# Ten state rows turned by ScalarE and TensorE, three C products on VectorE, and one state copy per pair of scans

## The chip, the cores and the metric

The kernel runs on one core of a Trainium2 chip. A core has five engines with a queue of their own each, worked off strictly in order: TensorE (PE: matrix products and transposes, results in PSUM), VectorE (DVE), ScalarE (ACT), GpSimd (POOL, which works on SBUF only in this kernel) and SyncE (SP, which issues nearly all DMAs). The metric is the device time of one launch in microseconds. Before the change it is 3146.35 us, the median of three runs from 3142.82 to 3151.95.

## The reference

The input `x` is (4, 512, 32, 32) in float32. Layer 0 normalises it by groups of channels and runs a selective state-space block over the 1024 pixels of each image; layer 1 is a block with two 3x3 convolutions and an attention over pixels. Only the recurrence of layer 0 matters to the change:

```python
xm, z = split(layernorm(tokens) @ W_in)               # 1024 channels each
xs = silu(causal_conv4(xm) + conv_b)
proj = xs @ W_x                                       # dt (32), B (16), C (16) per token
dt = softplus(proj[..., :32] @ W_dt + b_dt)
A = -exp(A_log)                                       # 1024 channels x 16 states
def step(h, inp):                                     # over the 1024 tokens
    dt_t, B_t, C_t, x_t = inp
    h = exp(dt_t * A) * h + (dt_t * x_t) * B_t        # h: channels x 16 states
    y = einsum('bds,bs->bd', h, C_t)
    return h, y
out = ((ys + xs * D_param) * silu(z)) @ W_out
```

## The kernel before, in words

**Tiling.** Channels lie on the 128 partitions, tokens along the free axis. A batch image has 8 chunks of 128 channels (`NDC`), taken two at a time (`e` = 0 to 3, `j` = 0, 1), and 1024 tokens, taken in two halves of 512 (`h` = 0, 1). So there are 4 x 4 x 2 = 32 groups `(b, e, h)`, and each holds 16 units, one for each state `s`. That makes 512 units and, with the two chunks, 1024 scans.

**One unit** (`unit`, L729 on). Each unit multiplies dt times x (`dtx`) by B, scans, multiplies by C and adds to y. B and C vary along the tokens and are the same on all partitions. The B product has two ways:

- *B on ScalarE* (`s in B_ON_ACT`): `dtx` has been transposed once per group (`dtxt`, tokens on partitions). ScalarE scales four pairs of rows by B (`sc`, L758, four instructions of 128x256), and TensorE turns them back into PSUM (`u`, L784, eight transposes). The decay exp(dt A) goes into an SBUF tile `da` of the ring `h` (L746).
- *B on GpSimd* (the other states): SP loads B spread over all partitions (`bbc`, 256 KB, L767), GpSimd multiplies (`dbx`, L773, 128x1024), and the decay goes into PSUM (`u`).

The scan over 512 tokens is one VectorE instruction per chunk (L798). In the half `h` = 0 a copy of the last element follows each scan (L803), into `carry_sb`, from which the scan of `h` = 1 starts. The C product again has two ways. For most states GpSimd multiplies both chunks at once by the loaded C (`cbc`, L820). For `s in C_ON_DVE` the scan writes to PSUM instead, and VectorE multiplies each chunk (L814, 128x512). Last, TensorE adds the result to `y` by transposing matmuls (L827, eight of 128x128).

**Rings.** `h` has 4 buffers for the states with B on ScalarE, `dbx` 4 for the others, `u` 4 PSUM banks, `sc` 2, `cbc` 6, `bb` 3. A buffer of `h` or `dbx` is free when TensorE has added it to `y`.

**The order of work.** `Plan` (L47 on) holds every piece of layer 0 as a step with an engine, an assumed duration in us, a priority, and the buffers it reads and writes. `issue` replays these durations and each time issues, among the steps that could start within `SLACK` of the soonest, the one of lowest priority number. So the order in every queue follows the assumed durations (`SCAN`, `EXP`, `ROWS`) and the priorities, which `PRM` spreads for the work beside the units: the next batch's normalisation (`m0`, `nl`), its projections and convolution taps (`q0`, `qg` for batch 1; `c0`, `cg` later), its parameters (`p0`), gates (`gates`), the previous batch's output projection (`o0`, `og`), the first image of layer 1 (`fi`), and, as filler, 32 weight transforms for layer 1 (`transform`, L1092 to L1106 on GpSimd). A step is only ordered here; at run time its engine waits on semaphores for whatever is not yet done, and everything behind it waits too.

Of the kernel before, what the change touches and what calls it, by code (L numbers as in the profile page):

```python
# [21 lines left out]
NS = 16  # L22
RK = 32
T = 512
# [3 lines left out]
GS = 16  # L28


PRM = dict(fi=0.66, m0=45.27, n0=50.77, nl=2.07, q0=63.18, qg=6.23, c0=53.17, cg=7.07, p0=122.02, e0=6.38, eg=3.72, g0=78.98, gg=9.04, o0=14.48, og=5.23, dl=9.01, t0=10, tg=21.42)


class Buf:
# [21 lines left out]
class Plan:  # L56
# [2 lines left out]

    ENGINES = ("PE", "DVE", "ACT", "POOL", "SP")  # L60
    LAG = {"PE": 0.2, "DVE": 0.08, "ACT": 0.1, "POOL": 0.06, "SP": 0.0}
    HOP, LOAD, SLACK, AHEAD = 0.05, 1.3, 0.07, 17.64

    def __init__(self, slots, in_order):
        self.slots, self.steps = dict(slots), []
# [104 lines left out]
def mamba_then_pab_kernel(  # L170
# [25 lines left out]
    nc = tc.nc  # L196
# [67 lines left out]
    with ExitStack() as l0:  # L264
# [10 lines left out]
        NPC = NCC * C // QC  # L275
        halves = [slice(h * T, (h + 1) * T) for h in range(NH)]

        B_ON_ACT = (0, 2, 4, 6, 8, 10, 12, 14, 15)

        C_ON_DVE = (1, 5, 9, 13)  # L280

        mean_w = wp.tile([P, P], F32, tag="mean_w", name="mean_w")
        nc.vector.memset(mean_w, 1.0 / C)
# [53 lines left out]
        )  # L337
        step = plan.step
        MM, TR = 0.88, 0.114
        ROWS, EXP, SCAN = 0.8, 0.62, 1.13  # L340

        def buf(ring, shape, name, free=False):
            if ring is None:
# [14 lines left out]

        proj = [buf(None, proj_sb[k * NP : (k + 1) * NP], "") for k in range(2)]
        bts = [buf(None, bt_sb[k], "") for k in range(2)]  # L360
        carry = [[buf(None, None, "") for j in range(2)] for s in range(NS)]
        bcds = [buf(None, t, "") for t in bcd]
        szds = [[buf(None, None, "") for d in range(NDC)] for b in range(B)]
        gds = [[[buf(None, None, "") for h in range(NH)] for k in range(2)] for b in range(B)]
# [319 lines left out]
        def delta(b, e, h, prio):  # L684

            pr = proj[b % 2]
            hs = halves[h]
            name = f"{b}_{e}_{h}"
            dt = buf("dt", [P, 2, T], f"dt_{name}")
            for j in range(2):  # L690
                d = 2 * e + j
                wd = wdt_sb[b % 2][:, d * P : (d + 1) * P]
                pd = group(f"pd_{name}_{j}", [(lambda wd=wd: wd, lambda: proj_sb[:, hs], [pr])], prio)
                step(
                    "ACT", 0.58,
                    lambda d=d, j=j, pd=pd: nc.scalar.activation(
                        dt()[:, j], pd(), AF.Identity, bias=bdt_sb[:, d : d + 1]
                    ),
                    [pd], [dt], prio,
                )  # L700
            step(
                "ACT", 0.97, lambda: nc.scalar.activation(dt(), dt(), AF.Softplus),
                [], [dt], prio, "softplus",
            )
            dtx = buf("dtx", [P, 2, T], f"dtx_{name}")
            us = [xs[b, 2 * e + j] for j in range(2)]

            def times():
                for j in range(2):
                    nc.gpsimd.tensor_mul(dtx()[:, j], dt()[:, j], us[j]()[:, hs])  # L710

            step("POOL", 2.37, times, [dt, *us], [dtx], prio)
            dtxt = buf("dtxt", [P, NK, 2, P], f"dtxt_{name}")
            for j in range(2):
                pt = buf("mm", [P, NK, P], f"pdt_{name}_{j}")

                def turn(j=j, pt=pt):
                    for k in range(NK):
                        nc.tensor.transpose(pt()[:, k, :], dtx()[:, j, k * P : (k + 1) * P], ident)

                step("PE", 4 * TR, turn, [dtx], [pt], prio)
                step(
                    "ACT", 0.48, lambda j=j, pt=pt: nc.scalar.copy(dtxt()[:, :, j, :], pt()),
                    [pt], [dtxt], prio,
                )
            dts[b, e, h] = dt, dtx, dtxt

        def unit(b, e, h, s, y):


            dt, dtx, dtxt = dts[b, e, h]
            hs = halves[h]
            name = f"{b}_{e}_{h}_{s}"
            prio = (b * NDC + 2 * e + h) * NS + s
            bc = bcds[b]
            c_bc = buf("cbc", [P, 1, T], f"cbc_{name}")
            step(
                "SP", 0.32,
                lambda: nc.sync.dma_start(c_bc()[:, 0], bcd[b][NS + s][hs].partition_broadcast(P)),
                [bc], [c_bc], prio, kb=256,  # L740
            )
            us = [buf("u", [P, T], f"u_{name}_{j}") for j in range(2)]

            def decay(j, t):
                at = (2 * e + j) * NS + s
                nc.scalar.activation(t, dt()[:, j], AF.Exp, scale=a_sb[:, at : at + 1])  # L746

            on_act, on_dve = s in B_ON_ACT, s in C_ON_DVE
            if on_act:
                bt = bts[b % 2]  # L750
                sc = buf("sc", [P, NK, 2, P], f"sc_{name}")
                hc = buf("h", [P, 2, T], f"da_{name}")
                for r in range(2):

                    def rows(r=r):
                        for k in range(2 * r, 2 * r + 2):
                            at = h * NK + k
                            nc.scalar.activation(  # L758
                                sc()[:, k], dtxt()[:, k], AF.Copy, scale=bt()[:, at, s : s + 1]
                            )  # L760

                    step("ACT", ROWS, rows, [dtxt, bt], [sc], prio)
            else:
                b_bc = buf("bb", [P, 1, T], f"bbc_{name}")
                step(
                    "SP", 0.32,
                    lambda: nc.sync.dma_start(b_bc()[:, 0], bcd[b][s][hs].partition_broadcast(P)),  # L767
                    [bc], [b_bc], prio, kb=256,
                )
                hc = buf("dbx", [P, 2, T], f"dbx_{name}")  # L770
                step(
                    "POOL", 2.31,
                    lambda: nc.gpsimd.tensor_mul(hc(), dtx(), b_bc().to_broadcast([P, 2, T])),  # L773
                    [dtx, b_bc], [hc], prio,
                )

            parts = [buf(None, None, "") for j in range(2)]
            for j, u in enumerate(us):
                part = parts[j]
                if on_act:  # L780

                    def turn(j=j, u=u):
                        for k in range(NK):
                            nc.tensor.transpose(  # L784
                                u()[:, k * P : (k + 1) * P], sc()[:, k, j, :], ident
                            )

                    step(
                        "ACT", EXP, lambda j=j: decay(j, hc()[:, j]), [dt], [part], prio, "exp",
                        holds=[hc],  # L790
                    )
                    step("PE", 4 * TR, turn, [sc], [u], prio - 1)
                else:
                    step("ACT", EXP, lambda j=j, u=u: decay(j, u()), [dt], [u], prio - 1, "exp")

                def scan(j=j, u=u):
                    ht = u() if on_dve else hc()[:, j]
                    nc.vector.tensor_tensor_scan(  # L798
                        ht, *((hc()[:, j], u()) if on_act else (u(), hc()[:, j])),
                        carry_sb[:, j, s : s + 1] if h else 0.0, ALU.mult, ALU.add,  # L800
                    )
                    if h == 0:
                        nc.vector.tensor_copy(carry_sb[:, j, s : s + 1], ht[:, T - 1 : T])  # L803

                step(
                    "DVE", SCAN if h else SCAN + 0.07, scan,
                    [part, u, *([carry[s][j]] if h else [])] if on_act
                    else [hc, u, *([carry[s][j]] if h else [])],
                    [u if on_dve else part, *([] if h else [carry[s][j]])], prio - 1, holds=[hc],
                )  # L810
                if on_dve:
                    step(
                        "DVE", 0.6,
                        lambda j=j, u=u: nc.vector.tensor_mul(hc()[:, j], u(), c_bc()[:, 0]),  # L814
                        [u, c_bc], [part], prio, holds=[hc],
                    )
            if not on_dve:
                step(
                    "POOL", 2.31,
                    lambda: nc.gpsimd.tensor_mul(hc(), hc(), c_bc().to_broadcast([P, 2, T])),  # L820
                    [c_bc], parts, prio, holds=[hc],
                )
            for j in range(2):

                def add(j=j):
                    for k in range(NK):
                        nc.tensor.matmul(  # L827
                            y[j]()[:, k, :], hc()[:, j, k * P : (k + 1) * P], ident,
                            start=(s == 0 and k == 0), stop=(s == NS - 1 and k == NK - 1),
                            is_transpose=True, skip_group_check=True,  # L830
                        )

                step("PE", 4 * TR, add, [parts[j]], [y[j]], prio, holds=[hc])
# [712 lines left out]
```

## Time and profile before

| | |
|---|---|
| median of three runs | 3146.35 us |
| profiled execution, its own time | 3149.88 us |
| its span | 3148.1 us (1.8 us of launch around it) |
| granted TensorE clock | 0.965 |
| start, before the first units | 0 to about 140 us |
| layer 0, units | about 140 to 2094 us |
| layer 1 | about 2094 to 3148 us |

The units end with the copy of the last `y` at 2093.68 to 2095.1 us. To read such a profile, look at each stage by itself: the shares of busy time over the whole span mix a stage in which four engines share the work with one in which TensorE does nearly all. An instruction's duration here includes a latency that the next one on the same engine can overlap. Where the cost of one more is wanted, the busy time of a group divided by its count, or the distance between starts in the timeline, is the better number. The "idle before" of a group and the list of waits name what ended an idle stretch.

### The profile page before, as it was taken

How to read it: one execution, taken by the hardware profiler on the slowest of the kernel's cores; microseconds unless marked ns; L12 is line 12 of the kernel's file. 1: busy time of each engine (PE TensorE's matmuls, PEld its weight loads, DVE VectorE, ACT ScalarE, POOL GpSimd, SP SyncE). 2: the span in 40 equal slices, each digit the busy share in tenths (PEclk: the TensorE clock that was granted, in tenths of full speed). 3: DMA queues.
4: the chain of work that ended last, by engine and by line, in shares of the span. 5: the costliest groups of instructions: out<-in, count | busy, mean ns of one | idle time of the engine just before them, and what ended most of it. 6: DMA issues, size and time to landing. Idle time of an engine off the chain costs nothing. (4 is left out here: it accounts for less than half of the span.)

```text
span 3148.1 us, 36186 instructions
## 1 busy us (share of the span) xinstructions
PE 2791.6 (89%) x11576; PEld 1642.3 (52%) x11576; DVE 2314.3 (74%) x3018; ACT 1859.4 (59%) x3198; POOL 2181.9 (69%) x1207
## 2 busy tenths in 40 slices
PE   4988789989889999888899877779999999999998
PEld 2455556656556656566656555444444444444443
DVE  3488999979998988898987888877285365447344
ACT  3499889997789998789998776652030030030000
POOL 8899997899978899978899998763152142224222
PEclk9999999999899999999999989989999999999999
DMA  6667555488645578745567654357268448628816
GB/s 195 194 188 216 152 159 166 142 249 242 208 122 168 173 214 248 227 127 163 162 193 222 212 179 127 118 146 262 92 233 313 175 158 309 254 82 308 318 68 245
DMA packets 406021, 608.41 MB, mean 193 GB/s; under 512 B 47688, under 2 KB 242504, under 8 KB 381256
## 3 DMA queue, kind: packets, MB, share of 16 engines
q1 hardware_dynamic: 396736, 590.52, 59.0%
q10 hardware_dynamic: 8936, 15.31, 1.3%
q8 instruction: 93, 1.52, 0.2%
q14 instruction: 96, 0.79, 0.1%
q0 software_dynamic: 160, 0.26, 0.0%
HBM read 508.99 MB, written 96.99 MB: 192 GB/s over the span
## 5 line engine op out<-in xcount | busy, mean ns | idle before, releaser
L820 POOL TENSOR_TENSOR da<-da,cbc 128x1024 f32<-128x1024 f32 x288 | 680.6, 2367 | 106.2 <-DVE carry_sb L803 54.3
L773 POOL TENSOR_TENSOR dbx<-dtx,bbc 128x1024 f32<-128x1024 f32 x224 | 528.6, 2371 | 24.8 <-DMA bbc<-bcd 10.8
L758 ACT ACTIVATE sc<-dtxt,bt_sb 128x256 f32<-128x256 f32 x1152 | 504.5, 497 | 48.0 <-PE u L784 46.8
L746 ACT ACTIVATE da<-dt,a_sb 128x512 f32<-128x512 f32 x576 | 394.3, 713 | 60.8 <-PE y L827 60.3
L784 PE MATMUL u<-ident,sc 128*128 128x128 f32 x2304 | 353.8, 286 | 72.5 <-DVE da L798 46.5
L798 DVE TENSOR_TENSOR_SCAN da<-da,carry_sb,u 128x512 f32<-128x512 f32 x288 | 356.2, 1263 | 73.6 <-PE u L784 71.1
L798 DVE TENSOR_TENSOR_SCAN da<-da,u 128x512 f32<-128x512 f32 x288 | 349.1, 1212 | 43.6 <-PE u L784 41.0
L827 PE MATMUL y<-ident,da 128*128 128x128 f32 x2304 | 326.4, 287 | 59.8 <-POOL da L820 56.5
L784 PEld LDWEIGHTS u<-ident,sc 128*128 128x128 f32 x2304 | 277.1, 146 | 181.2 <-DVE da L798 50.7
L827 PEld LDWEIGHTS y<-ident,da 128*128 128x128 f32 x2304 | 276.4, 147 | 163.1 <-POOL da L820 122.0
L1383 PE MATMUL m_b<-uw_b,v_b 128*128 128x512 f32 x768 | 336.0, 594 | 10.3 <-DMA uw_b<-u_b 8.6
L746 ACT ACTIVATE u<-dt,a_sb 128x512 f32<-128x512 f32 x448 | 299.0, 682 | 66.9 <-DVE da L798 34.5
L1383 PE MATMUL m_o<-uw_o,v_o 128*128 128x512 f32 x768 | 333.6, 595 | 4.8 <-DVE v_o L1305 4.1
L827 PE MATMUL y<-ident,dbx 128*128 128x128 f32 x1792 | 269.6, 289 | 54.6 <-DVE dbx L814 37.4
L827 PEld LDWEIGHTS y<-ident,dbx 128*128 128x128 f32 x1792 | 214.2, 148 | 124.3 <-DVE dbx L814 45.7
L381 PE MATMUL pxm<-xt,winc 128*128 128x344 f32 (+2 forms) x768 | 246.6, 468 | 21.0 <-ACT xt L557 8.1
L381 PE MATMUL pz<-xt,winc 128*128 128x512 f32 x512 | 246.9, 602 | 7.6 <-DVE xs L610 3.1
L1383 PEld LDWEIGHTS m_b<-uw_b,v_b 128*128 128x128 f32 x768 | 143.5, 190 | 195.9 <-issue 186.4
L820 POOL TENSOR_TENSOR dbx<-dbx,cbc 128x1024 f32<-128x1024 f32 x96 | 227.2, 2367 | 26.7 <-DVE carry_sb L803 13.7
L1383 PEld LDWEIGHTS m_o<-uw_o,v_o 128*128 128x128 f32 x768 | 145.9, 191 | 191.3 <-issue 184.0
L1431 PE MATMUL pat<-y_b,st 128*128 128x512 f32 x512 | 221.7, 593 | 0.1
L610 DVE SCALAR_TENSOR_TENSOR xs<-pxm,cw_sb,xs 128x341 f32<-128x341 f32 (+4 forms) x288 | 163.7, 570 | 56.9 <-ACT xs L601 50.0
(228 smaller groups left out, 4376.4 us busy)
## 6 DMA issues: line engine op xcount, KB each, us to landing
cbc<-bcd SPq DMA_DIRECT2D x512, 256.0 KB, 3.7
uw_b<-u_b SPq DMA_DIRECT2D x96, 1024.0 KB, 4.8
uw_o<-u_o SPq DMA_DIRECT2D x96, 1024.0 KB, 4.9
bbc<-bcd SPq DMA_DIRECT2D x224, 256.0 KB, 3.9
u_b<-work SPq DMA_DIRECT2D x192, 128.0 KB, 2.4
u_o<-work SPq DMA_DIRECT2D x192, 128.0 KB, 2.7
winc<-in_w_in_dram SPq DMA_DIRECT2D x64, 256.0 KB, 3.9
szd<-sz SPq DMA_DIRECT2D x32, 512.0 KB, 4.1
```

The lines of the kernel that those rows point to most:

```text
L381: lambda k=k, lhs=lhs, rhs=rhs: nc.tensor.matmul(p()[:, at : at + cols], lhs(), rhs(), start=(k == 0), stop=(k == n - 1)),
L610: nc.vector.scalar_tensor_tensor(u()[:, first:end], p()[:, first - k - at + before : end - k - at + before], cw[k], u()[:, first:end], ALU ...
L746: nc.scalar.activation(t, dt()[:, j], AF.Exp, scale=a_sb[:, at : at + 1])
L758: nc.scalar.activation(sc()[:, k], dtxt()[:, k], AF.Copy, scale=bt()[:, at, s : s + 1])
L773: lambda: nc.gpsimd.tensor_mul(hc(), dtx(), b_bc().to_broadcast([P, 2, T])),
L784: nc.tensor.transpose(u()[:, k * P : (k + 1) * P], sc()[:, k, j, :], ident)
L798: nc.vector.tensor_tensor_scan(ht, *((hc()[:, j], u()) if on_act else (u(), hc()[:, j])), carry_sb[:, j, s : s + 1] if h else 0.0, ALU.mul ...
L820: lambda: nc.gpsimd.tensor_mul(hc(), hc(), c_bc().to_broadcast([P, 2, T])),
L827: nc.tensor.matmul(y[j]()[:, k, :], hc()[:, j, k * P : (k + 1) * P], ident, start=(s == 0 and k == 0), stop=(s == NS - 1 and k == NK - 1), ...
L1383: nc.tensor.matmul(m[q], v[:, q, k, c, :], w[:, c, :], start=(c == 0), stop=(c == NCC - 1 and not extra),)
L1431: nc.tensor.matmul(pt, st[m][:, 2 * P * j + h : 2 * P * (j + 1) : 2], xb[m // 2][:, m % 2, :], start=(m == 0), stop=(m == NMC - 1),)
```

## The change

Three things are changed. After a pair of scans in `h` = 0, one copy takes both chunks' last elements (128x2), except for states with the C product on VectorE, which keep a copy per chunk. State 7 joins `B_ON_ACT` (nine states become ten), and `C_ON_DVE` goes from the states 1, 5, 9, 13 to 1, 6, 11. State 6 is in both lists. The planner's assumed durations and several priorities change, so that the order in all queues changes too.

```diff
-PRM = dict(fi=0.66, m0=45.27, ..., nl=2.07, q0=63.18, qg=6.23, ..., p0=122.02, ..., og=5.23, ...)
+PRM = dict(fi=4.61, m0=27.7, ..., nl=1.39, q0=50.1, qg=7.76, ..., p0=120.48, ..., og=4.13, ...)
-    HOP, LOAD, SLACK, AHEAD = 0.05, 1.3, 0.07, 17.64
+    HOP, LOAD, SLACK, AHEAD = 0.05, 1.3, 0.05, 17.64
-        B_ON_ACT = (0, 2, 4, 6, 8, 10, 12, 14, 15)
-        C_ON_DVE = (1, 5, 9, 13)
+        B_ON_ACT = (0, 2, 4, 6, 7, 8, 10, 12, 14, 15)
+        C_ON_DVE = (1, 6, 11)
-        ROWS, EXP, SCAN = 0.8, 0.62, 1.13
+        ROWS, EXP, SCAN = 0.8, 0.61, 1.18
-        carry = [[buf(None, None, "") for j in range(2)] for s in range(NS)]
+        carry = [buf(None, None, "") for s in range(NS)]
-            step("POOL", 2.37, times, [dt, *us], [dtx], prio)
+            step("POOL", 2.46, times, [dt, *us], [dtx], prio)
-                    if h == 0:
+                    if h == 0 and on_dve:
                         nc.vector.tensor_copy(carry_sb[:, j, s : s + 1], ht[:, T - 1 : T])
-                step(
-                    "DVE", SCAN if h else SCAN + 0.07, scan,
-                    [part, u, *([carry[s][j]] if h else [])] if on_act
-                    else [hc, u, *([carry[s][j]] if h else [])],
-                    [u if on_dve else part, *([] if h else [carry[s][j]])], prio - 1, holds=[hc],
-                )
+                before, behind = ([carry[s]], []) if h else ([], [carry[s]] if on_dve else [])
+                step(
+                    "DVE", SCAN + (0.15 if behind else 0.0), scan,
+                    [part if on_act else hc, u, *before],
+                    [u if on_dve else part, *behind], prio - 1, holds=[hc],
+                )
...
+            if h == 0 and not on_dve:
+                step(
+                    "DVE", 0.15,
+                    lambda: nc.vector.tensor_copy(carry_sb[:, :, s], hc()[:, :, T - 1]),
+                    parts, [carry[s]], prio - 1, holds=[hc],
+                )
```

More of the change, by code (lines that the diff above doesn't have):

```diff
@@ L28 @@
 GS = 16
-PRM = dict(fi=0.66, m0=45.27, n0=50.77, nl=2.07, q0=63.18, qg=6.23, c0=53.17, cg=7.07, p0=122.02, e0=6.38, eg=3.72, g0=78.98, gg=9.04, o0=14.48, og=5.23, dl=9.01, t0=10, tg=21.42)
+PRM = dict(fi=4.61, m0=27.7, n0=50.77, nl=1.39, q0=50.1, qg=7.76, c0=53.17, cg=7.07, p0=120.48, e0=6.38, eg=3.72, g0=78.98, gg=9.04, o0=14.48, og=4.13, dl=9.01, t0=10, tg=21.42)
 class Buf:
```

## The prediction, made before the changed kernel ran

> **What bounds the kernel now.** I read the page's busy times and its 40 slices first, then busy time by stretches, the groups by shape, the waits inside the stage of the units, and pieces of the timeline.
>
> ```profile
> PE   4988789989889999888899877779999999999998
> DVE  3488999979998988898987888877285365447344
> ACT  3499889997789998789998776652030030030000
> POOL 8899997899978899978899998763152142224222
> ```
>
> A slice is 78.7 us. Up to slice 26 (2094 us) four engines are near full together; after it TensorE alone is. The change touches nothing after it. The last copies of y recur at the same place every 492 us, so I cut the units into half batches: four groups (e = 0, 1), then four (e = 2, 3). Columns of this view: length, then busy us of PE, PE loads, DVE, ACT, POOL, the granted clock, DMA.
>
> ```profile
> 140.00:395.00 255.00, 207.38 (x1075) 139.72 (x1074) 204.90 (x276) 232.13 (x398) 235.84 (x134) 0.92 0.63 188
> 395.00:645.00 250.00, 229.02 (x1189) 152.13 (x1188) 226.71 (x313) 228.86 (x379) 218.97 (x120) 0.98 0.54 163
> 645.00:891.00 246.00, 212.16 (x1150) 147.31 (x1148) 220.72 (x300) 204.28 (x367) 238.40 (x127) 0.94 0.71 216
> 891.00:1137.00 246.00, 225.68 (x1146) 148.71 (x1146) 219.35 (x300) 224.93 (x373) 206.57 (x109) 0.98 0.54 163
> ...
> 1629.00:1861.00 232.00, 198.47 (x1059) 136.76 (x1057) 196.32 (x252) 186.88 (x335) 218.09 (x114) 0.93 0.68 214
> 1861.00:2094.00 233.00, 176.63 (x971) 120.79 (x972) 202.29 (x266) 152.35 (x284) 193.22 (x96) 0.95 0.47 131
> ```
>
> Three regimes show (batch 2, left out, repeats batch 1). In a **first half** GpSimd is busy 238 of 246 us: it is the bound. In a **second half**, with the next batch's projections and taps, PE, ACT and DVE are at 92, 91 and 89% and none is alone. In the **last half** nothing is projected any more and DVE leads (202 of 233). Who waits, from 140 to 2090 us (total us, times, longest):
>
> ```profile
> DVE da L798 <- PE u L784: 112.1, 47, 20.5
> ...
> ACT da L746 <- PE y L827: 60.3, 40, 5.1
> PE y L827 <- POOL da L820: 54.6, 60, 3.3
> POOL da L820 <- DVE carry_sb L803: 54.3, 33, 5.4
> ```
>
> The engines wait in a ring: GpSimd for the copy behind the second scan, TensorE for GpSimd's C product, ScalarE for TensorE to free an `h` buffer, VectorE for transposes queued behind all that. The chain of waits over the last 215 us of the units is mostly scans. I price from these rows (busy, mean ns):
>
> ```profile
> L758 ACT ACTIVATE sc<-dtxt,bt_sb 128x256 f32<-128x256 f32 x1152 | 504.5, 497 | 48.0 <-PE u L784 46.8
> L784 PE MATMUL u<-ident,sc 128*128 128x128 f32 x2304 | 353.8, 286 | 72.5 <-DVE da L798 46.5 <-ACT sc L758 9.7 <-ACT dt L696 4.2
> L814 DVE TENSOR_TENSOR dbx<-u,cbc 128x512 f32<-128x512 f32 x256 | 168.7, 675 | 0.0
> ```
>
> and a scan's pitch from the timeline:
>
> ```profile
> 927.70 1.22 DVE L798 TENSOR_TENSOR_SCAN u<-u,dbx 128x512 f32<-128x512 f32 x1
> 928.96 0.16 DVE L803 COPY carry_sb<-u 128x1 f32<-128x1 f32 x1
> 929.03 1.22 DVE L798 TENSOR_TENSOR_SCAN u<-u,dbx 128x512 f32<-128x512 f32 x1
> ...
> 2081.90 2.44 DVE L798 TENSOR_TENSOR_SCAN u<-u,carry_sb,dbx 128x512 f32<-128x512 f32 x2
> 2084.25 1.25 DVE L798 TENSOR_TENSOR_SCAN da<-da,carry_sb,u 128x512 f32<-128x512 f32 x1
> ```
>
> With a copy a scan takes 929.03 - 927.70 = 1.33 us from start to start; without one, (2084.25 - 2081.90) / 2 = 1.175. A copy so costs 0.155 us of VectorE.
>
> [...] a one-element copy takes 154 ns. So a copy of two elements should cost as one. [...] scans of 1269 ns mean (u, h = 1) at a pitch of 1.175 us, which is why I use pitches. [...] the trace has 1283 ns and no drain (a load at 911.55 starts 0.02 us after the work before it, and its exp at 912.84), so I use 1.283.
>
> **The change part by part.**
>
> *VectorE.* Copies: 13 states lose one of two in each of 16 groups with h = 0, 208 x 0.155 = -32.2 us. One C state less: 2 x 32 = 64 products x 168.7/256 = 0.659, -42.2 us. Sum -74.4, or -9.3 in each of eight half batches. State 6 scans from SBUF and PSUM into PSUM, a mix without a row; the nearest scans are 1212 and 1225 ns, 13 ns x 64 is under 1 us either way, so nothing.
>
> *GpSimd.* C products 12 to 13 states: +32 x 2.367 = +75.7. B products 7 to 6: -32 x 2.371 = -75.9. Nothing remains. But the filler moves: in the two programs' GpSimd queues, 12.3 transforms stand among units with e = 0, 1 before and 11.0 after, the rest going to second halves. One transform is (70.0 + 69.9 + 69.9 + 58.2 + 58.2 + 58.0)/32 = 12.0 us (six GpSimd rows of x96 and x32), so 16 us leave the four first halves, 4 each, and go where GpSimd idles 31 to 39.
>
> *ScalarE.* State 7: 4 x 32 = 128 scalings x 504.5/1152 = 0.438, +56.1; its 64 exps go to SBUF (394.3/576 against 299.0/448 us), +1.1; the changed order has 67 table loads for the exp instead of 71, -5.1. Sum +52.1, +6.5 per half.
>
> *TensorE.* 8 x 32 = 256 transposes x 353.8/2304 = 0.154, +39.3, or +4.9 per half.
>
> *SP.* 32 loads of B (256 KB, 8.4 MB of 608) and their 32 issues go. The DMAs are busy 61% in the stage and no wait of this kind leads, so nothing; bounds 0 and -11 us, all the waits of GpSimd for `bbc` (10.8 us).
>
> *Waits.* GpSimd's C product waited for the second copy; it now waits for the single one. In the changed order 161 of 208 stand directly behind their second scan, 47 one to five instructions later. At one scan of 1.2 us those cost up to 56 us of lateness, spread over 16 groups; behind each waits GpSimd's queue, then TensorE's y. Against it, every unit with h = 0 is ready 0.155 us sooner, and the plan assumes for a pair of scans with its copy 2 x 1.18 + 0.15 = 2.51 us, which the pitches above bear out (2 x 1.175 + 0.155), where it took 2 x 1.20 for a real 2.66. I set these against each other at zero; alone they are -54 us (all of GpSimd's waits for `carry_sb`) and +20. The other priorities reorder mostly batch 1's projections: zero, bounds -10 and +10.
>
> *The sum.* First halves are paid by GpSimd: -2 in batch 0 (ACT is beside it at 232), -4 in batches 1 and 2, -3 in batch 3: -13. Second halves of batches 0 to 2: VectorE gives 9.3, ScalarE and TensorE take 6.5 and 4.9 into idle stretches of about 21: zero, bounds -8 and +6.5 each. Last half: VectorE paces it, -9. Together **-22 us** on the profiled execution's 3149.88; that stands 3.5 above the median, so about **3124 us**.
>
> **Rivals.**
>
> 1. *ScalarE and TensorE become the bound in second halves.* If their idle 21 us can't be entered, because `h` (four buffers) now serves ten states instead of nine and exps wait more for TensorE's y, each of three halves grows by 6.5; with first halves unchanged and late copies eating the last half's gain, +20: about 3166. For it: 60.3 us of ScalarE's waits are for a free `h`. Against: 36.7 of them fall in batch 3, where ScalarE is busy 65 to 80%. It decides where ScalarE's busy time passes about 231 of 246 and the half gets longer.
> 2. *GpSimd alone paces all.* Its work is the same; freed VectorE time turns to idle. 0 to -5, about 3144. For it: 238 of 246. Against: only in first halves.
> 3. *VectorE paced more than its share shows*, through the carry waits. All of 9.3 in five halves (second halves and the last two) and 5 in the other three: -62, about 3085. For it: GpSimd's longest waits in a second half are for the copy (5.2 us at 895). Against: DVE idles 27 us there.
>
> That the copy doesn't merge is excluded: the order shows 208 of 128x2 and 96 of 128x1 for 512.
>
> **Numbers.** Forecast with rival 3: 0.52. Rival 1: 0.33. Rival 2 and small sums: 0.15. The likeliest is 3124. From rival 3's 3085 to a little past rival 1 gives 3085 to 3175; alone the forecast would be 3100 to 3144. A difference of 0.3% (9 us) is about what a measurement of this kernel can tell from no change: faster 0.52, same 0.15, slower 0.33.
>
> **What would show it.** Right: first halves of 242 us or less, GpSimd still near 97%; second halves near 246 with ScalarE at 231, DVE at 210; last half near 224; carry waits under 54 us. Wrong: second halves over 250, ScalarE's waits for y well over 60 us, or a layer 1 that differs at all by over 5 us.

## The result, and the profile after

The changed kernel takes 3147.44 us, the median of 12 runs (3140.93 to 3152.20), against 3150.07 us for the kernel before in 12 runs: a ratio of 0.9995 with a 95% interval of 0.9986 to 1.0004. No change. The profiled execution has a span of 3150.4 us.

The page of after, the same four engines in 40 slices (78.8 us each) and the busy times. Nothing in the slices tells that any work was taken off VectorE:

```profile
PE 2801.1 (89%) x11832; PEld 1654.8 (53%) x11832; DVE 2324.9 (74%) x2746; ACT 1896.9 (60%) x3322; POOL 2185.6 (69%) x1207
...
PE   4988878989888999888999877779999999999998
DVE  3488899988999988999987987876275366447344
ACT  3499889998799999789998787752030030020000
POOL 8899898999969999978899998853052142224222
```

VectorE has 272 instructions fewer (3018 to 2746) and is busy 10.6 us *more* (2314.3 to 2324.9). That is the whole puzzle in one line. By half batches (columns as in the prediction; these cuts lie at the copies of y that end each half, to 1.5 us):

```profile
140.00:414.00 274.00, 231.20 (x1170) 157.35 (x1171) 217.30 (x261) 246.48 (x425) 240.29 (x137) 0.90 0.61 175
414.00:661.00 247.00, 219.02 (x1197) 147.03 (x1196) 225.02 (x267) 226.53 (x392) 224.92 (x122) 0.99 0.57 166
661.00:901.00 240.00, 207.40 (x1127) 141.12 (x1125) 220.48 (x257) 201.90 (x367) 228.66 (x123) 0.96 0.68 208
901.00:1150.00 249.00, 228.30 (x1216) 154.07 (x1214) 221.09 (x269) 235.16 (x398) 215.66 (x117) 0.99 0.54 162
...
1867.00:2096.00 229.00, 177.29 (x1001) 126.27 (x1002) 198.95 (x234) 158.80 (x297) 193.41 (x97) 0.94 0.50 129
```

Batch 0 is 10.7 us longer than before (it ends at 661.7 instead of 651.0), batches 1 to 3 are 0.9, 3.1 and 5.2 us shorter. Layer 1, from 2095 us on, is as it was (1054 against 1053 us). The groups by shape of after show where VectorE's time is:

```profile
L820 DVE COPY carry_sb<-da 128x2 f32<-128x2 f32 x144 | 83.8, 582 | 3.9
L820 DVE COPY carry_sb<-dbx 128x2 f32<-128x2 f32 x64 | 43.3, 676 | 1.6
L803 DVE COPY carry_sb<-u 128x1 f32<-128x1 f32 x96 | 15.2, 158 | 3.3
```

In the kernel before the same transfers were these:

```profile
L803 DVE COPY carry_sb<-da 128x1 f32<-128x1 f32 x288 | 44.3, 154 | 10.0
L803 DVE COPY carry_sb<-u 128x1 f32<-128x1 f32 x128 | 20.3, 158 | 4.4
L803 DVE COPY carry_sb<-dbx 128x1 f32<-128x1 f32 x96 | 14.8, 154 | 3.3
```

The copies of one element, from PSUM (`u`), take 158 ns as before. The merged ones of two elements, from SBUF (`da` and `dbx`), take 582 and 676 ns in the mean, where one element from SBUF took 154. All copies together were 44.3 + 20.3 + 14.8 = 79.4 us before, and are 142.3 us now, though there are 304 instead of 512.

The timeline of after shows one of the longest:

```profile
940.78 1.19 DVE L798 TENSOR_TENSOR_SCAN dbx<-u,dbx 128x512 f32<-128x512 f32 x1
942.01 2.37 DVE L820 COPY carry_sb<-dbx 128x2 f32<-128x2 f32 x1
944.29 1.21 DVE L798 TENSOR_TENSOR_SCAN da<-da,u 128x512 f32<-128x512 f32 x1
```

and GpSimd's at the same time:

```profile
939.67 4.68 POOL L826 TENSOR_TENSOR da<-da,cbc 128x1024 f32<-128x1024 f32 x2
944.45 2.36 POOL L826 TENSOR_TENSOR dbx<-dbx,cbc 128x1024 f32<-128x1024 f32 x1
```

The copy ends at 942.01 + 2.37 = 944.38, GpSimd's second product at 939.67 + 4.68 = 944.35. I laid the two timelines of after over each other for all 208 merged copies. 70 last over 0.5 us, and each of these ends within 0.04 us of the end of a GpSimd instruction. Of the 117 that last up to 0.25 us, 38 start while GpSimd is idle and 77 in the last 0.25 us of its instruction; two start together with it. Turned round: 77 start inside a GpSimd instruction that has over 0.25 us left, and 76 of them end with it, one with the next. In the kernel before 254 copies of one element from SBUF start so, and none takes over 0.16 us. This time is inside the instruction's duration: the two groups have 3.9 and 1.6 us of idle time before them, and no list of waits shows the rest.

### The profile page after: what moved, and what is told of

It reads as the page before. It is cut to its first block, busy times and chain, and to the rows that moved or that the text cites. A ratio compares the mean times of both kernels' runs of the same rounds, so it can differ in the third digit from the quotient of the medians.

```text
span 3150.4 us, 36613 instructions
## 1 busy us (share of the span) xinstructions
PE 2801.1 (89%) x11832; PEld 1654.8 (53%) x11832; DVE 2324.9 (74%) x2746; ACT 1896.9 (60%) x3322; POOL 2185.6 (69%) x1207
## 5 line engine op out<-in xcount | busy, mean ns | idle before, releaser
L826 POOL TENSOR_TENSOR da<-da,cbc 128x1024 f32<-128x1024 f32 x288 | 679.4, 2364 | 87.2 <-DVE carry_sb L820 47.4
L758 ACT ACTIVATE sc<-dtxt,bt_sb 128x256 f32<-128x256 f32 x1280 | 557.1, 496 | 49.3 <-PE u L784 48.8
L746 ACT ACTIVATE da<-dt,a_sb 128x512 f32<-128x512 f32 x640 | 439.4, 713 | 70.1 <-PE y L833 69.5
L773 POOL TENSOR_TENSOR dbx<-dtx,bbc 128x1024 f32<-128x1024 f32 x192 | 452.1, 2367 | 30.6 <-DMA bbc<-bcd 8.3
L784 PE MATMUL u<-ident,sc 128*128 128x128 f32 x2560 | 380.6, 282 | 52.4 <-DVE da L798 31.7
L833 PE MATMUL y<-ident,da 128*128 128x128 f32 x2560 | 357.3, 283 | 70.7 <-POOL da L826 68.2
L784 PEld LDWEIGHTS u<-ident,sc 128*128 128x128 f32 x2560 | 302.2, 144 | 160.3 <-issue 41.7
L826 POOL TENSOR_TENSOR dbx<-dbx,cbc 128x1024 f32<-128x1024 f32 x128 | 302.8, 2365 | 32.1 <-DVE carry_sb L820 22.6
L746 ACT ACTIVATE u<-dt,a_sb 128x512 f32<-128x512 f32 x384 | 252.9, 679 | 34.8 <-DVE da L798 18.9
L833 PE MATMUL y<-ident,dbx 128*128 128x128 f32 x1536 | 217.1, 281 | 43.7 <-POOL dbx L826 31.6
L833 PEld LDWEIGHTS y<-ident,dbx 128*128 128x128 f32 x1536 | 178.4, 144 | 98.2 <-POOL dbx L826 48.6
```

The source lines that it names most:

```text
L758: nc.scalar.activation(sc()[:, k], dtxt()[:, k], AF.Copy, scale=bt()[:, at, s : s + 1])
L784: nc.tensor.transpose(u()[:, k * P : (k + 1) * P], sc()[:, k, j, :], ident)
L833: nc.tensor.matmul(y[j]()[:, k, :], hc()[:, j, k * P : (k + 1) * P], ident, start=(s == 0 and k == 0), stop=(s == NS - 1 and k == NK - 1), ...
```

## The experiments

I began with three theories of the zero. **S**: the shifted projections of batch 1 cost batch 0 its 10.7 us, and a lighter VectorE gave the rest back. **L**: VectorE's work is worth nothing, only the order differs. **M**: the merged copies that stand behind other work delay GpSimd. After the first four runs two more came up: **P**, a copy of more than one element between SBUF tiles waits for the instruction that GpSimd is running, and **W**, it waits for the scan before it or for its stride. Each ratio below is to the kernel before, run on the same chip; a change in us is the ratio times 3149.

**Planner constants alone** (e1_plan_only), on the program before: the new `PRM`, `SLACK`, `EXP`, `SCAN` and the 2.46.

```diff
-PRM = dict(fi=0.66, m0=45.27, ...)
+PRM = dict(fi=4.61, m0=27.7, ...)
-                    "DVE", SCAN if h else SCAN + 0.07, scan,
+                    "DVE", SCAN if h else SCAN + 0.15, scan,
```

> The program before (nine B states, four C states, a copy per chunk) with the planner constants of after: PRM, SLACK, EXP, POOL 2.46, SCAN 1.18 and for h = 0 SCAN + 0.15. No engine's work changes, only the order. Theory S (the shifted projections of batch 1 cost batch 0 its 10.7 us, the lighter VectorE gives 9 us back later): batch 0 ends some 10 us later than before and nothing is given back, total +8 to +15, about 3155 to 3163. Rival L (VectorE's work is worth nothing anywhere, all differences between the two traces come from the order): total near that of after, 3144 to 3152. Rival M (the merged copies that stand behind other work eat the gain): no merged copy here, so no loss, 0 to -10.

Measured: 1.0061 (1.0048 to 1.0074), +19 us. All three theories expected less. And batch 0 ends at 654.1, only 3 us late; the loss comes later, most of it in batches 1 and 3. S gave the wrong place.

**The changed kernel with the old priorities** (e2_after_old_prm).

```diff
-PRM = dict(fi=4.61, m0=27.7, ...)
+PRM = dict(fi=0.66, m0=45.27, ...)
```

> The kernel after with the PRM line of before and nothing else changed. Theory S: batch 0 no longer loses, later batches keep their gain, -8 to -15 against before, 3132 to 3142. Rival L: the order of before comes back in large part, 3144 to 3152. Rival M: the late copies stay, so no gain, 3144 to 3155.

Measured: 1.0122 (1.0108 to 1.0136), +38 us. None had expected so large a loss. S falls here: the new priorities are not what eats a gain; without them the same program is slower by 40 us.

**The merge alone, at the order of before** (e3_merge_old_order). The transfer is issued inside the second scan's step, so every queue keeps its order.

```diff
-                    if h == 0:
+                    if h == 0 and on_dve:
                         nc.vector.tensor_copy(carry_sb[:, j, s : s + 1], ht[:, T - 1 : T])
+                    elif h == 0:
+                        scanned.append(j)
+                        if len(scanned) == 2:
+                            nc.vector.tensor_copy(carry_sb[:, :, s], hc()[:, :, T - 1])
```

> The kernel before with one change: in states without C on VectorE one copy of 128x2 directly behind the second scan replaces two of 128x1; planner costs and all queues' order otherwise as before, 32 us less on VectorE. Theory S: VectorE sets part of the pace, -5 to -15. Rival L: 0 within 4 us. Rival M: the merge without late copies gains what the forecast said of it, -10 to -20.

Measured: 1.0111 (1.0093 to 1.0129), +35 us, where all three expected a gain or nothing, and the forecast priced a saving. No copy is late here, so M doesn't explain it. Its groups:

```profile
L808 DVE COPY carry_sb<-da 128x2 f32<-128x2 f32 x144 | 81.4, 566 | 4.9
L808 DVE COPY carry_sb<-dbx 128x2 f32<-128x2 f32 x48 | 28.3, 590 | 1.6
L804 DVE COPY carry_sb<-u 128x1 f32<-128x1 f32 x128 | 20.3, 158 | 4.4
```

Copies take 130.0 us, 50.6 more than before.

**No copies at all** (e4_no_copies), order as before.

```diff
+        nc.vector.memset(carry_sb, 0.0)
...
-                    if h == 0:
-                        nc.vector.tensor_copy(carry_sb[:, j, s : s + 1], ht[:, T - 1 : T])
```

> The kernel before with all 512 copies left out (the scans of the second half of the tokens start from zero instead of the carried state), order of all queues otherwise as before; 512 x 0.155 = 79 us less on VectorE. This measures what VectorE time is worth at a fixed order. Theory S: -12 to -35. Rival L: 0 within 5 us. Rival M: as S, -20 to -40.

Measured: 0.9851 (0.9837 to 0.9865), -47 us for 79 us of copies off VectorE, more than S or M had. L falls: at the order of before, this time on VectorE is worth 0.6 us per us.

**The merged transfer as a reduce** (f1_after_reduce): the kernel after, one instruction exchanged, order the same.

```diff
-                    lambda: nc.vector.tensor_copy(carry_sb[:, :, s], hc()[:, :, T - 1]),
+                    lambda: nc.vector.reduce_max(carry_sb[:, :, s], hc()[:, :, T - 1 : T], axis=AX.X),
```

> The kernel after, its merged copy written as a maximum over an axis of length one (reduce, one SBUF input) in place of a copy; order as after. In the trace of after the 208 merged copies take 0.61 us in the mean, 0.16 to 2.67, where the copies of one element take 0.155. Theory P (a copy of an even number of elements between SBUF tiles [...] waits for the end of GpSimd's running instruction; a reduce doesn't): each merged state transfer falls to about 0.16, 208 x 0.45 = 94 us less on VectorE, and at the 46 us per 79 that e4_no_copies gained, -55 against after, about 3093 (3080 to 3115). Rival W (the wait is for the second scan's result to land or for the stride of 512 elements, not for GpSimd): the reduce takes as long as the copy, 3147. Rival L (order alone decides): within 5 us of after.

Measured: 3101.62 us, 0.9845 (0.9831 to 0.9860), -49 us. It beats both kernels. The groups by shape:

```profile
L820 DVE TENSOR_REDUCE carry_sb<-da 128x2 f32<-128x2 f32 x144 | 22.4, 155 | 3.9
...
L820 DVE TENSOR_REDUCE carry_sb<-dbx 128x2 f32<-128x2 f32 x64 | 9.9, 155 | 1.6
```

155 ns with the same two elements, the same stride and the same scan before it: W falls. And it runs beside GpSimd: 147 of the 208 reduces start inside a GpSimd instruction that has over 0.25 us left, and none takes over 0.17 us; in the timelines of this run a reduce takes 0.15 us at 935.31, while GpSimd is in the middle of a product that started at 933.87:

```profile
935.31 0.15 DVE L820 TENSOR_REDUCE carry_sb<-dbx 128x2 f32<-128x2 f32 x1
```

```profile
933.87 2.37 POOL L773 TENSOR_TENSOR dbx<-dtx,bbc 128x1024 f32<-128x1024 f32 x1
```

**The merge alone as a reduce** (f2_merge_reduce_old_order): e3 with this instruction.

> The kernel before with two copies of 128x1 merged into one reduce of 128x2, order of all queues as before; as e3_merge_old_order but for the instruction. Theory P: what the forecast priced, 192 x 0.155 = 30 us less on VectorE, at 0.58 us per us -17 against before, 3125 to 3138. Rival W: as e3, about +36, 3185. Rival L: the order is that of before, so 3148.

Measured: 0.9903 (0.9886 to 0.9920), -31 us for 28.8 us less in copies (50.6 against 79.4). More than P expected, and the answer to the forecast's own price: the merge is worth what was written, if the transfer doesn't wait.

**Two elements, and three** (f3_copy_two, f4_copy_three): before, with each copy taking the last two or three neighbouring elements, nothing else.

```diff
-                        nc.vector.tensor_copy(carry_sb[:, j, s : s + 1], ht[:, T - 1 : T])
+                        nc.vector.tensor_copy(carry_sb[:, j, s, 0:2], ht[:, T - 2 : T])
```

> The kernel before with its 512 copies of 128x1 made 128x2 (the last two neighbouring elements; the scan starts from the second), order as before. 384 of them read SBUF, 128 read PSUM. Theory P: those from SBUF rise to about 0.57 us in the mean, those from PSUM stay at 0.16; 384 x 0.42 = 160 us more on VectorE, +60 to +160, 3210 to 3310. Rival W: the stride is gone, all copies stay at 0.155, 3148. Rival L: 3148.

> As f3_copy_two with three elements, an odd number. Theory P with evenness as the condition: copies stay at 0.155 to 0.16 us, time as before, 3143 to 3153. If the condition is more than one element instead: as f3. Rivals W and L: 3148.

Measured: 1.0499 (1.0477 to 1.0522) and 1.0505 (1.0489 to 1.0520), +157 and +159 us. Groups of the run with two:

```profile
L803 DVE COPY carry_sb<-da 128x2 f32<-128x2 f32 x288 | 181.6, 631 | 9.9
...
L803 DVE COPY carry_sb<-dbx 128x2 f32<-128x2 f32 x96 | 60.3, 628 | 3.3
L803 DVE COPY carry_sb<-u 128x2 f32<-128x2 f32 x128 | 20.4, 160 | 4.4
```

and of the run with three:

```profile
L803 DVE COPY carry_sb<-da 128x3 f32<-128x3 f32 x288 | 178.4, 619 | 9.9
```

With one element more, the copies between SBUF tiles that begin beside a working GpSimd end with it: 198 of the 384 in the run with two start inside a GpSimd instruction that has over 0.25 us left, and all 198 end with it. Those from PSUM, in the same run, stay at 160 ns. The evenness that I had assumed is not the condition: three take as long as two (619 ns in the mean against 631 from `da`), where one takes 154.

**What is left: lists and priorities.** With the instruction mended, the other parts can be told apart. Four runs complete the table: the reduce with the old priorities (g1_reduce_old_prm, the `PRM` line of before in f1), the lists alone on before (g2_lists_only), the kernel after with a copy of one element per chunk (g3_after_two_copies) and f1 with the old lists (g4_reduce_old_lists).

```diff
# g3_after_two_copies, against after
-                    if h == 0 and on_dve:
+                    if h == 0:
-                before, behind = ([carry[s]], []) if h else ([], [carry[s]] if on_dve else [])
+                before, behind = ([carry[s]], []) if h else ([], [carry[s]])
...
-            if h == 0 and not on_dve:
-                step(
...
# g2_lists_only, against before (g4 is the reverse, against f1)
-        B_ON_ACT = (0, 2, 4, 6, 8, 10, 12, 14, 15)
-        C_ON_DVE = (1, 5, 9, 13)
+        B_ON_ACT = (0, 2, 4, 6, 7, 8, 10, 12, 14, 15)
+        C_ON_DVE = (1, 6, 11)
```

> f1_after_reduce with the PRM line of before. Against e2_after_old_prm (3187), which differs only in the instruction of the merged transfer, theory P expects about as much as the reduce gave elsewhere (46 us from after to f1, 63 from e3 to f2): 3124 to 3141. That the new priorities were what made up for the waiting copies (after 39 us below e2) would show as a difference to f1_after_reduce of about that size, 3135 to 3145; priorities that are only luck of the order, within 10 us of f1: 3092 to 3112.

> The kernel before with the two lists of after (ten states with B on ScalarE, C on VectorE for states 1, 6, 11), a copy per chunk and all planner constants as before. 42 us less on VectorE, 57 more on ScalarE, 39 more on TensorE. If VectorE sets the pace as e4_no_copies says (0.58 us per us): -15 to -25, 3125 to 3135. If ScalarE and TensorE become the bound in the second halves (the forecast's rival 1): +10 to +25, 3160 to 3175.

> The kernel after with a copy of 128x1 behind every scan of h = 0 in place of the merged copy of 128x2; lists and planner constants of after. Theory P: 208 waiting copies of 0.61 us (127 us) give way to 416 of 0.155 (64 us): -63 us on VectorE, about -30 against after at the 0.48 us per us that f1 gave: 3105 to 3130. If the merge as such is worth what the forecast said, this lies about 15 to 30 above f1_after_reduce.

> f1_after_reduce with the two lists of before (nine states, four C products on VectorE). Against f1 it has 42 us more on VectorE, 57 less on ScalarE, 39 less on TensorE. If the lists help through VectorE: 3115 to 3130. If they only trade one load for another: within 8 us of f1, 3094 to 3110.

Change against before in us, with what the kernel has:

| lists | priorities | copies of one element | merged reduce | merged copy |
|---|---|---|---|---|
| old | old | 0 | -31 (f2) | +35 (e3) |
| new | old | +28 (g2) | -7 (g1) | +38 (e2) |
| old | new | +19 (e1) | -10 (g4) | not run |
| new | new | -12 (g3) | -49 (f1) | -2 (after) |

In e2 and g1 only the `PRM` line is old, the other planner constants are those of after; in g2 all are old. The intervals of the last four are 0.9970 to 0.9984 (g1), 1.0077 to 1.0103 (g2), 0.9950 to 0.9977 (g3) and 0.9956 to 0.9981 (g4). Read along a row, the reduce gains 29 to 37 us over two copies, and the merged copy loses 10 to 35. Only in the first row is the order of the queues strictly the same; in the others it moves with the form of the transfer. Read down, lists and priorities each lose alone and gain together: new lists cost 28 under the old priorities and bring 31 under the new ones (19 to -12). So the lists' sign depends on the order.

Against what was expected, g1 lies at 3139.94 us, at the end of P's range and inside the one for priorities that matter (3135 to 3145). g2, at 3177.21, is just above what was written for a bound on ScalarE and TensorE. g3, at 3138.93, misses its 3105 to 3130: it has 47 us less on VectorE than after (2277.9 against 2324.9) and gains 10 us. g4, at 3137.98, misses both of its ranges: the old lists cost 39 us against f1. So the 0.6 us per us of e4 can't be carried over to another order.

Of g2's loss, by the copies of y, 22 us lie in the first halves (12 of them in batch 0's) and 11 in the second halves of batches 0 to 2; the last half gains 4. ScalarE is busy 5 to 9 us longer in these second halves. GpSimd's waits for the scans rose most among its own (48.5 us for `da` from VectorE, against 20.1 before). Load and order are not told apart there, and the cause stays open.

## Why the prediction was wrong, point by point

**The step that failed** is the first term of its sum: "So a copy of two elements should cost as one", and from it 208 x 0.155 = -32.2 us. The mis-sized term measured +62.9 us (142.3 against 79.4), 95 us off. I took the price from the pitch beside a 128x1 copy: the one at 928.96 lasts 0.16 us, and the next scan starts at 929.03, 0.09 us before its end. This holds here (copies of one element take 158 ns in after as before), and the reduce of two elements does cost 155 ns. That a copy of two would cost as one was my estimate from copies of one; no trace had shown it. But the instruction's *form* had changed, and in the runs the time goes with form and operands: copies between SBUF tiles take 619 to 632 ns in the mean with two or three elements (f3, f4) and 154 with one, those from PSUM 160 with two (f3), the reduce of two 155 (f1). What in the hardware makes the difference was not shown. What was shown is the match in time: of the 208 merged copies in after, 91 last over 0.25 us, and all 91 end with a GpSimd instruction. No run took GpSimd's work away. The forecast called GpSimd's work unchanged, which in all it was; it didn't ask what GpSimd's being busy 97% of a half does to a neighbour.

**The other terms of work** came near on VectorE and GpSimd, and smaller than written on ScalarE and TensorE. C products: 84.0 + 41.9 = 125.9 us, -42.8 for the forecast -42.2. ScalarE's scalings: 557.1 - 504.5 = +52.6 for +56.1; all of ScalarE +37.5 for +52.1. TensorE's transposes: 380.6 - 353.8 = +26.8 for +39.3. GpSimd: 2181.9 to 2185.6, nothing, as written. State 6's mixed scans take 1219 and 1265 ns, no price of their own.

**How a load becomes time** was wrong in both kinds of halves. Of the 74 us off VectorE the sum let 9 count, in the last half; the 13 us of the first halves came from GpSimd's filler, and the second halves stood at zero. At the order of before the runs give 47 us per 79 us of copies (e4), 31 per 29 (f2), 35 per 51 (e3) and 157 per 183 (f3): 0.6 to 1.1. To see where, I cut at the copies of y. The forecast's cuts, 246 us apart, lay 4 to 8 us beside them and hid that in the kernel before a first half takes 232 us and a second 258. e4 takes 79 / 8 = 9.9 us of copies from each half and changes no order. Batch 1 in before and in e4:

```profile
651.00:883.10 232.10, 201.60 (x1080) 139.26 (x1078) 209.34 (x282) 190.99 (x344) 225.59 (x122) 0.94 0.73 221
883.10:1141.20 258.10, 234.10 (x1209) 155.78 (x1210) 229.31 (x316) 236.35 (x393) 217.90 (x116) 0.98 0.54 161
```

```profile
643.70:874.50 230.80, 202.37 (x1080) 141.94 (x1078) 199.38 (x218) 190.17 (x344) 225.18 (x123) 0.93 0.73 223
874.50:1122.50 248.00, 230.43 (x1209) 156.70 (x1210) 219.26 (x253) 234.51 (x393) 217.16 (x115) 0.98 0.56 168
```

The first half gains 1 us, and GpSimd fills it (225 of 231): that GpSimd paces it held. The second half, put at zero, gains the whole 10, although ScalarE is busy 235 of its 248 us. By halves, in us against before:

| | forecast | after | f1 | e4 |
|---|---|---|---|---|
| four first halves | -13 | +24.5 | 0 | -6 |
| three second halves | 0 | -19 | -40 | -27 |
| last half | -9 | -4 | -10 | -10 |

So "second halves: zero" was the second mis-sized term. The -13 failed too. The filler didn't leave the first halves: its transforms take 151 us in the four of them before and 148 in after, and GpSimd as a whole is busy 905 us there before and 911 in after. Of their +24.5 us in after, 17 lie in batch 0's. e1, in which no work changes, has 12 there; this part goes with the order, for which the forecast had zero within 10 us, and what in the order does it was not followed. The -9 of the last half came where the transfer doesn't wait.

**The waits.** "Carry waits under 54 us" was the sign to watch: GpSimd's for `carry_sb` are 47.4 us on the `da` tiles, which that 54 stood for, but 22.6 on `dbx`, 70.0 in all, where they were 54.3 + 13.7 = 68.0. The forecast had left out the 13.7. I had blamed a possible failure on the 47 late copies (in the trace of after, as in its queue, 161 of the 208 stand directly behind a scan); f1 has them at the same places and gains 49 us.

**The rivals.** The measured time is rival 2's, but not for its reason: GpSimd doesn't pace all. It lies where a loss by a waiting instruction (after against g3, +10) meets a gain of the rest (g3, -12). Rival 1 is out as the cause of the zero: it needed longer second halves, and those of batches 0 to 2 are 6 to 7 us shorter in after. Its sign of 231 us for ScalarE says nothing, since by the copies of y ScalarE was already busy 236 of 258 us before. In g2 these halves do grow, by 1, 1 and 9 us; rival 1 may be part of it there. Rival 3's 62 us come nearer to f1's 49 than the forecast's 22 do.

**Layer 1** is unchanged, as written.

## What to carry to other kernels

Merging small instructions gained here only in a form that doesn't wait: at the order of before the merge brought 31 us as a reduce (f2) and cost 35 as a copy (e3). A VectorE copy of two or three float32 elements per partition between SBUF tiles took 0.57 to 0.68 us in the mean, where one element takes 0.154; all 91 of after that took over 0.25 us, and all 198 of f3 that began with over 0.25 us of a GpSimd instruction to go, ended with GpSimd's instruction. A reduce over an axis of length one moved two elements in 0.155 us, and never took over 0.17 beside a busy GpSimd. Larger copies were not tried. Look at an instruction's duration by shape, not only at the lists of waits: the merged copies' 127.1 us in after (83.8 + 43.3) count as busy time, whatever part of it is a wait. Measure a part at a fixed order of the queues before judging it together with a new order; here lists and priorities each lose alone and gain together.

## What the runs showed that I had not expected

- In after a 128x2 copy between SBUF tiles takes 0.16 to 2.67 us, 0.61 in the mean; each that takes over 0.25 us ends within 0.04 us of the end of a GpSimd instruction. GpSimd's own products keep their length (2364 ns against 2367).
- A copy of three elements takes as long as one of two (619 against 631 ns, f4 and f3); of the copies of one element from SBUF in before none takes over 0.16 us (154 ns in the mean).
- 183 us more in waiting copies (f3) cost 157 us of the kernel. VectorE's 74% over the span hides how little slack it has among the units: there it is busy 1709 of 1954 us before, and 1889 of 2122 in f3.
